# A graph layer on one core: ScalarE's column picks in three loads, turned data and the norm in steps without a layer

## The chip, the core and the metric

The kernel runs on 1 core of one Trainium2 chip. The core's engines have their own instruction streams, each in order, and wait for each other by semaphores: TensorE (PE; its weight loads are PEld), VectorE (DVE), ScalarE (ACT), GpSimd (POOL) and SyncE (SP, which only issues transfers). The metric is the device time of one execution in microseconds (us), lower is better; the number compared is the median of several runs.

## What is computed

One layer of an equivariant graph network on 12500 nodes of 128 features, with 412500 edges sorted by their target node `dst`, then a residual and a layer norm. The essence of the reference:

```python
f0 = x0 @ W1_0e / sqrt(MUL);  f1 = einsum('nui,uw->nwi', x1, W1_1o) / sqrt(MUL)
feat0, self0 = f0[:, :MUL], f0[:, MUL:];  feat1, self1 = f1[:, :MUL], f1[:, MUL:]
e0, e1 = feat0[edge_src], feat1[edge_src]                 # a gather for each edge
h = gelu(gelu(edge_scalar_attr @ W_mlp1 / sqrt(8)) @ W_mlp2 / sqrt(64))
w00, w01, w10, w11 = h @ Wp_00, h @ Wp_01, h @ Wp_10, h @ Wp_11
out0_a = w00 * e0 * ea0
out0_b = w11 * sum(e1 * ea1[:, None, :], -1) / sqrt(3)
out1_a = (w01 * e0)[:, :, None] * ea1[:, None, :]
out1_b = w10[:, :, None] * e1 * ea0[:, :, None]
n0, n1 = segment_sum(mid0, edge_dst), segment_sum(mid1, edge_dst)   # mid = concat(out) / sqrt(2)
y = [cos * self0 + sin * (n0 @ W2_0e), cos * self1 + sin * einsum(n1, W2_1o)]
out = layernorm(x + y)
```

## The kernel before

**Tiling.** The edges are cut into 806 *runs* of 512 (4 columns `q` of 128 edges) and the runs into 202 *chunks* of 4. The nodes are cut into 25 *groups* of 512 for the features before the edges and the norm behind them; the last group has 212.

**Start.** A loop over the groups loads x (SP), turns it on PE into `xT`, which stays in SBUF for the whole kernel, multiplies it by the weights `wf`, and stores the features to `table` in DRAM from ACT's queue (`store_nodes`, line 260). Meanwhile POOL gathers the rows of the first 18 runs from x itself (72 gathers); these are turned and multiplied later (`turn_rows`, `features`). The small loads (weights, first node of each chunk, and `tile_first`, the first target node of each 128 edges, in tiles `tf`) leave SP's queue one in each turn of that loop (line 925). `tile_places` (DVE) turns `tf` into offsets. Loads that are needed later stand in the list `late` and leave SP's queue in the main loop, 12 a step.

**Main loop.** Step `s` treats run `s`, with `c, k = divmod(s, 4)`. The order of the work on each engine is written out by hand (`tc.manual_schedule`): the program order of a step is what each engine does.

- POOL: `gather(s + 18)` (line 222), one indirect DMA for each column of 128 edges, from `table` into one of 19 buffers `G`. Some columns are left out because another engine makes them:
- DVE and ACT *pick columns*: for 128 edges they copy 128 columns of `xT` one by one into a tile `gt` (`pick_nodes` loads the addresses into registers, line 178; `pick` copies, line 190 on DVE and 192 on ACT). PE multiplies the tile by `wf` (line 198) and ACT copies the result to `G` (`picked_rows`, 199). `SLOTS` says how many columns each engine takes in each slot of a run: DVE 32 on average in three slots, ACT 28 in two (12 and 16). Each 128 columns save POOL one gather. SP makes one column in 14 runs with single-row transfers (`aid`).
- PE: the edge weights of coming runs (`weights`, 569), the segment sums of run `s - 1` into PSUM (`segments`, 666 and 668), and the edge network two chunks ahead: `radial` turns the edge data (527, ACT copies it out in 529), `mlp1` (536, ACT's gelu in 540), `mlp2` (551 and 556). `radial` stands in step k = 0, `mlp1` in k = 1, `mlp2` in k = 3. `turn_attributes` (521, 523) comes once in 32 runs. These small products share two PSUM buffers named `h`.
- DVE: the messages `M` of run `s` (637, 641), the indicator `own` of the next chunk (`select`, 616 and 630, which also reads one element of each gathered piece, 597), and the addition of a finished chunk's sums to the accumulator `acc` (681), which covers 768 nodes.
- Norm: `due` names the chunk after which a group is complete. Then `norm` does the group's products on PE (`moments`, 698 and 701), ACT copies them to `y` (706) and moves the remaining accumulator columns to the other `acc` buffer (`move_sums`, 428); DVE clears the rest of it piece by piece (425). Before the change this stands in step k = 3 of the next chunk, beside `mlp2`. `norm_on` (statistics, 714) and `norm_end` (normalise on ACT, 742, and a store from SP's queue, 260) follow for two groups at a time in steps 1 and 2 of the chunk after.

**End.** The last two groups, 23 and 24, are complete only with the last chunks; `end` marks the last two chunks, where the norm's steps stand earlier.

Of the kernel before, what the change touches and what calls it, by code (L numbers as in the profile page):

```python
# [50 lines left out]
SLOTS = {DVE: [(12, 12, 0), (12, 12, 8), (12, 12, 8), (12, 12, 16)], ACT: [(12, 16)]}  # L51
# [7 lines left out]
def gnn_kernel(ctx: ExitStack, tc: tile.TileContext, x, src, dst, ea4, ea8, w1_0, w1_1, wm1, wm2,  # L59
# [277 lines left out]
    def weight_loads():  # L337

        yield w1r, sub(wm1, 0, [[0, P // RAD], [HID, RAD], [1, HID]])
        yield w2b, sub(wm2, 0, [[0, 2], [HID, HID], [1, HID]])  # L340
        for j, w in enumerate((wp00, wp01, wp10, wp11)):
            yield wpb[:, j * MUL:(j + 1) * MUL], sub(w, 0, [[0, 2], [MUL, HID], [1, MUL]])
        for t, w in ((w20, w2_0), (w21, w2_1)):
            yield t[:MUL, :], w[:MUL, :]
            yield t[MUL:, :], sub(w, MUL * MUL, [[0, 3], [MUL, MUL], [1, MUL]])
        yield first_node, sub(dst, 0, [[1, 1], [CH * SB, NCH]])
        for b, t in enumerate(tile_first):
            c0, n = b * P, t.shape[0]
            last = c0 + n == NCH and E < NCH * CH * SB
            if last:  # L350
                yield (t[n - 1:n, :].rearrange("a (k o) -> a k o", o=1),
                       sub(dst, (NCH - 1) * CH * SB, [[1, 1], [0, CH * Q], [1, 1]]))
                k = -(-(E - (NCH - 1) * CH * SB) // P)
                yield t[n - 1:n, :k], sub(dst, (NCH - 1) * CH * SB, [[k * P, 1], [P, k]])
            yield t[:n - last], sub(dst, c0 * CH * SB, [[CH * SB, n - last], [P, CH * Q]])
# [37 lines left out]
    NT = -(-NCH // P)  # L393
    tile_first = [cst.tile([min(P, NCH - b * P), CH * Q], I32, name=f"tf{b}") for b in range(NT)]
# [12 lines left out]

    def tile_places():

        for b, t in enumerate(tile_first):  # L410
# [234 lines left out]
    def places(c):  # L645

        b, r = divmod(c, P)
# [37 lines left out]
    before_last = due[NCH - 1][0] - 1  # L685

    def moments(b, sums=None):
        n0, nn, full, tail, tiles = group(b)
        if not pend:
# [3 lines left out]
        j = len(pend)  # L693
        pend.append(b)
        pt = ps.tile([P, XB, P], F32, name="h")
        at = n0 - base[-1] if b in due[NCH - 1] else 0
        for t, k in tiles:
# [5 lines left out]
            else:  # L703
                nc.vector.tensor_tensor(pt[:k, t, :], pt[:k, t, :], sums[:k, t, :], op=OP.add)
        if full:
            nc.scalar.activation(Y["y"][:, j, :full, :], pt[:, :full, :], AF.Copy)
        if tail:
            nc.scalar.activation(Y["y"][:tail, j, full, :], pt[:tail, full, :], AF.Copy)

    def statistics(b):  # L710
        j = pend.index(b)
        st = wk.tile([P, XB, 6], F32, name="bst")
        for t, k in group(b)[4]:
            nc.vector.bn_stats(st[:k, t, :], Y["y"][:k, j, t, :])
# [8 lines left out]
    def normalise(last=False, keep=False):  # L723
# [9 lines left out]
        for j, b in enumerate(pend):  # L733
            if b in done:
                continue
            for t, k in group(b)[4]:
                i = j * XB + t - i0
                if last and t % 2:
                    nc.vector.tensor_scalar(y[:k, j, t, :], y[:k, j, t, :], r[:k, i:i + 1], m[:k, i:i + 1],
                                            op0=OP.mult, op1=OP.add)  # L740
                    continue
                nc.scalar.activation(y[:k, j, t, :], y[:k, j, t, :], AF.Identity,  # L742
                                     bias=m[:k, i:i + 1], scale=r[:k, i:i + 1])
            store_nodes(nc.sync, out, b, y[:, j])
# [4 lines left out]
    def norm(bs):  # L749
        for b in bs:  # L750
            moments(b)
# [14 lines left out]
    def norm_last(bs):  # L766
# [6 lines left out]
        if len(pend) > len(done):  # L773
            deviations()
            normalise(True)

# [119 lines left out]
    with tc.manual_schedule(engines={PE, ACT, DVE, SP}):  # L896
# [7 lines left out]
        for b in range(min(AHEAD, NG)):  # L904
# [9 lines left out]
                 NG // 2 + 9: tile_places, NG // 2 + 10: lambda: mlp2(1), NG // 2 + 11: make_ws, NG: make_wpost}  # L914
# [20 lines left out]
        late = list(aid_load())  # L935
# [10 lines left out]
        for s in range(NCH * CH + CH):  # L946
# [7 lines left out]
            if s % P == P // 2 and (s // P + 1) * P < NS:  # L954
# [10 lines left out]
            pick(ACT, P)  # L965
            pick_nodes(ACT, s, 1)
# [39 lines left out]
            if k == 1 and 1 < c < NCH:  # L1006
                norm_on(due.get(c - 2, []))
            if k == 2 and 1 < c < NCH - 1:
                norm_end(due.get(c - 2, []))
            if k == 0 and c == NCH:  # L1010
                norm_end(due.get(c - 3, []))
                norm_on(due.get(c - 2, []))
                norm_end(due.get(c - 2, []))
# [12 lines left out]
            if s == 2:  # L1026
                nc.vector.memset(owns[1], 0.0)
            if s == 5:
# [38 lines left out]
```

## Time and profile before

| | us |
|---|---|
| median of 3 runs (lowest to highest) | 3556.44 (3555.64 to 3560.35) |
| the profiled execution's own time | 3556.29 |
| its span, first to last instruction | 3554.4 |

A line of a group in the profile reads: line, engine, operation, output<-inputs, shape, count, then busy time in us and the mean ns of one, then the engine's idle time just ahead of them and what ended it. A line of the timeline has the start, the busy time, engine, line, operation and in brackets the idle time ahead with its releaser. A line of waits has the waiting group, what released it, total us, times and the longest. "issue" as a releaser means that the engine waited for nothing that the profile shows. ACTq, DVEq and SPq are the engines' own instruction issue (register loads, DMA starts).

### The profile page before, as it was taken

The page shows a single profiled execution, that of the slowest core. Times are in us where ns is not written, and L with a number is a line of the kernel's source. Part 1 is how long each engine was busy: PE and PEld are TensorE (multiplying, and loading weights), DVE is VectorE, ACT ScalarE, POOL GpSimd, SP SyncE. Part 2 cuts the span into 40 slices and gives each one's busy share as a digit, 9 for nine tenths or more (in the row PEclk, how much of TensorE's full clock was granted, in tenths as well). Part 3 has the DMA queues.
Part 4 walks back from the last instruction along what each step waited for, and adds up shares of the span by engine and source line. Part 5 has one row for each costly group of instructions (what it writes and reads, how often), then busy time and mean ns, then how long its engine had stood idle before and what let it go on. Part 6 is the DMA issues. An engine that isn't in the chain of part 4 may idle for free. (4 is left out here: it accounts for less than half of the span.)

```text
span 3554.4 us, 143693 instructions
## 1 busy us (share of the span) xinstructions
PE 3159.9 (89%) x28598; PEld 2755.6 (78%) x28598; DVE 3129.2 (88%) x29317; ACT 2797.6 (79%) x23671; POOL 2667.6 (75%) x2804
## 2 busy tenths in 40 slices
PE   6899898998898988998899898898899989888888
PEld 6777777787777777877788787787787777777777
DVE  2699999999999999999899899888899888889897
ACT  3488788788888888887887888877787887788785
POOL 7777777777777777777777777777777777777775
PEclk8999999998999999899998899989899999999998
DMA  8322332223322223322323323323323232232221
GB/s 199 70 62 68 63 64 65 63 61 74 64 60 67 63 60 74 64 60 62 68 61 70 67 59 64 65 63 68 65 62 64 59 69 63 60 69 63 60 65 47
DMA packets 579225, 239.29 MB, mean 67 GB/s; under 512 B 483651, under 2 KB 528747, under 8 KB 578347
## 3 DMA queue, kind: packets, MB, share of 16 engines
q0 software_dynamic: 89536, 183.55, 20.3%
q1 hardware_dynamic: 468041, 40.02, 9.1%
q10 hardware_dynamic: 20770, 6.47, 0.8%
q8 instruction: 252, 4.13, 0.5%
q14 instruction: 626, 5.13, 0.5%
HBM read 217.00 MB, written 12.80 MB: 65 GB/s over the span
## 5 line engine op out<-in xcount | busy, mean ns | idle before, releaser
L222 POOL DMA_INDIRECT G<-table,idx x2726 | 2598.9, 953 | 836.7 <-issue 718.5
L192 ACT ACTIVATE gt<-xT 128x1 f32 x22016 | 2166.7, 190 | 73.3 <-issue 53.6
L190 DVE COPY gt<-xT 128x1 f32 x25216 | 1728.6, 144 | 212.1 <-issue 172.9
L666 PE MATMUL sums<-own,M 128*128 128x96 f32 x6446 | 1354.8, 294 | 74.3 <-DVE M L641 73.0
L668 PE MATMUL sums<-own,M 128*128 128x96 f32 x6446 | 1319.7, 288 | 85.1 <-DVE M L641 84.1
L666 PEld LDWEIGHTS sums<-own,M 128*128 128x128 f32 x6446 | 1037.5, 201 | 181.9 <-DVE M L641 101.7
L668 PEld LDWEIGHTS sums<-own,M 128*128 128x128 f32 x6446 | 1035.3, 202 | 108.9 <-DVE M L641 107.6
L641 DVE TENSOR_TENSOR M<-w,G 128x384 f32<-128x384 f32 x1612 | 880.1, 547 | 0.0
L569 PE MATMUL w<-wpb,h 64*128 64x128 f32 x6448 | 649.3, 305 | 57.8 <-DVE M L641 56.3
L569 PEld LDWEIGHTS w<-wpb,h 64*128 64x128 f32 x6448 | 496.5, 197 | 199.6 <-issue 74.3
L637 DVE TENSOR_TENSOR M<-w,G 128x256 f32<-128x256 f32 x806 | 333.4, 414 | 34.4 <-issue 19.9
L540 ACT ACTIVATE h<-h 128x512 f32<-128x512 f32 x404 | 216.3, 586 | 178.6 <-PE h L536 165.7
L536 PE MATMUL h<-eT,w1b 64*128 64x128 f32 x3232 | 288.7, 319 | 8.4 <-ACT e L523 8.3
L536 PEld LDWEIGHTS h<-eT,w1b 64*128 64x128 f32 x3232 | 241.3, 218 | 38.7 <-ACT e L523 13.7
L556 ACT ACTIVATE h<-h 128x512 f32<-128x512 f32 x404 | 213.5, 577 | 26.3 <-PE h L551 22.5
L551 PE MATMUL h<-h,w2b 64*64 64x256 f32 x3232 | 222.6, 391 | 0.0
L199 ACT ACTIVATE G<-h 128x128 f32<-128x128 f32 x369 | 96.4, 277 | 120.5 <-PE h L198 76.4
L198 PE MATMUL h<-wf,gt 128*128 128x128 f32 x738 | 143.5, 294 | 1.9 <-ACT h L556 0.9
L529 ACT ACTIVATE eT<-h 128x128 f32<-128x128 f32 x202 | 56.0, 277 | 112.7 <-PE h L527 89.5
L551 PEld LDWEIGHTS h<-h,w2b 64*64 64x64 f32 x3232 | 104.5, 133 | 44.8 <-issue 0.5
L630 DVE TENSOR_TENSOR own<-oh,e 128x512 f32<-128x512 f32 x202 | 137.6, 681 | 0.7 <-issue 0.2
L681 DVE TENSOR_TENSOR acc<-sums,acc 128x384 f32 x202 | 111.2, 550 | 9.7 <-issue 6.2
(113 smaller groups left out, 1329.1 us busy)
## 6 DMA issues: line engine op xcount, KB each, us to landing
G<-table SPq DMA_DIRECT2D x7168, 0.5 KB
G<-table,idx POOLq DMA_INDIRECT x2726
e<-in_edge_attr SPq DMA_DIRECT2D x201, 64.0 KB
own<-in_x SPq DMA_DIRECT2D x24, 256.0 KB
table<-acc ACTq DMA_DIRECT2D x24, 256.0 KB
xt<-in_edge_attr SPq DMA_DIRECT2D x24, 256.0 KB
out<-y SPq DMA_DIRECT2D x24, 256.0 KB
xt<-in_dst SPq DMA_DIRECT2D x5, 256.0 KB
```

What stands on the lines that cost most here:

```text
L190: nc.vector.tensor_copy(to, col)
L192: nc.scalar.activation(to, col, AF.Copy)
L222: nc.gpsimd.indirect_dma_start(out=G[s][:, q, :], out_offset=None, in_=x if s < raw_runs else table, in_offset=bass.IndirectOffsetOnAxis(a ...
L536: nc.tensor.matmul(p1[h][:, j // 2, j % 2, :], w1b[rows, j, :], eT[c][rows, :], start=True, stop=True)
L540: nc.scalar.activation(H1[c][h], p1[h].rearrange("p k j e -> p (k j e)"), AF.Gelu_apprx_tanh, scale=1.0 / math.sqrt(RAD))
L551: nc.tensor.matmul(p2[r][k * HID:(k + 1) * HID, h * n:(h + 1) * n], w2b[rows, :], H1[c][h][rows, k * n:(k + 1) * n], start=True, stop=True)
L556: nc.scalar.activation(H2[c][r].rearrange("p k j e -> p (k j e)"), p2[r], AF.Gelu_apprx_tanh, scale=1.0 / math.sqrt(HID))
L569: nc.tensor.matmul(WP[i][:, q, :], H2[c][q % 2][rows, k, q // 2, :], wpb[rows, :], start=True, stop=True)
L637: nc.vector.tensor_tensor(M[s][:, :, :, :MUL], w[:, :, :2 * MUL].rearrange("p q (a u) -> p q a u", a=2), g[:, :, None, :MUL].to_broadcast( ...
L641: nc.vector.tensor_tensor(M[s][:, :, j, MUL:].rearrange("p q (i u) -> p q i u", i=3), w[:, :, None, (2 + j) * MUL:(3 + j) * MUL].to_broadc ...
L666: nc.tensor.matmul(flat[:, bass.ds(at, 4 * FIRST_HALF)].bitcast(F32), M[s][:, q, 0, :], own[:, 3 * WIDE:], start=False, stop=False)
L668: nc.tensor.matmul(sb[:, 1:, bass.ds(at, 4 * WIDE)].bitcast(F32), M[s][:, q, 1, :], own[:, :3 * WIDE].rearrange("p (a j) -> p a j", a=3), ...
```

## The change

1. ACT picks 28 and 32 columns by turns, in three slots: (12, 8, 8) and (12, 8, 12). The third slot's addresses are loaded ahead of the layer, its columns are copied behind it.
2. `radial` goes to step k = 2, one chunk further ahead; `turn_attributes` from the 21st to the 24th run of 32 (k = 0); `load_indices` two steps on.
3. The norm's products go to step k = 0 of the second chunk behind (`norm_products`), its copy and `move_sums` to k = 1 (`norm_keep`); the first clearing is in that same step. Statistics and end move to k = 2 of the third and k = 0 of the fourth chunk behind.
4. The products of group 23 are done by tiles of 128 nodes as soon as each is complete (`done_at`), so that one of four is left for the end; `find_first` keeps later edges from writing to finished tiles. The products of group 24 stay in PSUM and are normalised from there; its tiles are stored one by one from two queues.
5. `tile_first` is cut into tiles of 16, 128 and 58 chunks. The first is loaded first of the start's small loads, the other two behind the loads of `late`; their `tile_places` come in run 9.

```diff
-SLOTS = {..., ACT: [(12, 16)]}
+SLOTS = {..., ACT: [(12, 8, 8), (12, 8, 12)]}
+FIRST_TILES = 16
...
     def weight_loads():
+        yield from tile_loads(0)
         yield w1r, sub(wm1, 0, [[0, P // RAD], [HID, RAD], [1, HID]])
...
-        for b, t in enumerate(tile_first):
-            c0, n = b * P, t.shape[0]
+    def tile_loads(b):
+        t, c0 = tile_first[b], tile_from[b]
...
+    tile_from = [0, *range(FIRST_TILES, NCH, P)]
+    NT = len(tile_from)
+    before_last = due[NCH - 1][0] - 1
+    done_at = [math.ceil((before_last * GN + (t + 1) * P + MARGIN) / N * NCH) - 1 for t in range(XB)]
...
+        for t, (a, z) in enumerate(zip(done_at, done_at[1:])):
+            nc.vector.tensor_scalar(strays[:, a + 1:z + 1], strays[:, a + 1:z + 1], float((t + 1) * P), None, op0=OP.max)
...
-    def moments(b, sums=None):
+    def moments(b, sums=None, part=None, hold=False):
         n0, nn, full, tail, tiles = group(b)
+        if part is not None:
+            tiles = tiles[part:part + 1]
...
+        if sums is None and b == NG - 1:
+            Y["pt"] = pt
+            return
+        if part is not None:
+            nc.scalar.activation(Y["y"][:, j, part, :], pt[:, part, :], AF.Copy)
+            return
+        if hold:
+            Y["held"] = Y["y"][:, j], pt
+            return
...
+                if last:
+                    eng = nc.sync if t % 2 else nc.scalar
+                    eng.dma_start(out[b * GN + t * P:b * GN + t * P + k, :], y[:k, j, t, :])
+            if not last:
+                store_nodes(nc.sync, out, b, y[:, j])
...
     def norm(bs):
         for b in bs:
-            moments(b)
+            moments(b, part=XB - 1 if b == before_last else None)
             move_sums()
             new_sums()
+    def norm_products(bs):
+        for b in bs:
+            moments(b, hold=True)
+    def norm_keep(bs):
+        for b in bs:
+            y, pt = Y.pop("held")
+            nc.scalar.activation(y, pt, AF.Copy)
+            move_sums()
+            new_sums()
...
-        late = list(aid_load())
+        late = list(aid_load()) + [load for b in range(1, NT) for load in tile_loads(b)]
...
             pick(ACT, P)
+            if k == 1 and 1 < c < NCH - 2:
+                norm_keep(due.get(c - 2, []))
+                clearing += [(c, a) for a in range(4)] if c - 2 in due else []
             pick_nodes(ACT, s, 1)
...
-            if k == 0 and c + 2 < NCH:
-                radial(c + 2)
-            if s % ET == 21 and s - 21 + ET < NS:
+            if s == 0:
+                radial(2)
+            if k == 2 and c + 3 < NCH:
+                radial(c + 3)
+            if s % ET == 24 and s - 24 + ET < NS:
                 turn_attributes(s // ET + 1)
...
+            pick(ACT, P)
+            pick_nodes(ACT, s, 2)
             if k % 2 and c + 2 < NCH:
-                pick(ACT, P)
                 (mlp1 if k == 1 else mlp2)(c + 2)
...
-            if k == 1 and 1 < c < NCH:
+            if k == 2 and 2 < c < NCH - 1:
+                norm_on(due.get(c - 3, []))
+            if k == 0 and 3 < c < NCH - 1:
+                norm_end(due.get(c - 4, []))
+            if k == 1 and c == NCH - 1:
                 norm_on(due.get(c - 2, []))
-            if k == 2 and 1 < c < NCH - 1:
-                norm_end(due.get(c - 2, []))
...
-            if k == (1 if end else 3) and 0 < c < NCH:
+            if k == 0 and 1 < c < NCH - 2:
+                norm_products(due.get(c - 2, []))
+            if k == 1 and c == NCH - 2:
                 norm(due.get(c - 1, []))
-                clearing += [(c, a) for a in range(4)] if c - 1 in due and not end else []
+            if k == 0 and (c - 3 == done_at[0] or c - 2 in done_at[1:-1]):
+                moments(before_last, part=0 if c - 3 == done_at[0] else done_at.index(c - 2))
...
+            if s == 9:
+                tile_places(range(1, NT))
```

More of the change, by code (lines that the diff above doesn't have):

```diff
@@ L392, in gnn_kernel @@
     first_at = cst.tile([1, NCH], I32)
-    NT = -(-NCH // P)
-    tile_first = [cst.tile([min(P, NCH - b * P), CH * Q], I32, name=f"tf{b}") for b in range(NT)]
+    tile_from = [0, *range(FIRST_TILES, NCH, P)]
+    NT = len(tile_from)
+    tile_first = [cst.tile([z - a, CH * Q], I32, name=f"tf{b}")
+                  for b, (a, z) in enumerate(zip(tile_from, tile_from[1:] + [NCH]))]
+    before_last = due[NCH - 1][0] - 1
+    assert len(due[NCH - 1]) == 1
+    done_at = [math.ceil((before_last * GN + (t + 1) * P + MARGIN) / N * NCH) - 1 for t in range(XB)]
+    assert due[done_at[-1]] == [before_last] and done_at == sorted(set(done_at))
+    assert not any(c in due for c in (*range(done_at[0] - 1, done_at[-1]), 0, NCH - 4, NCH - 2)) and done_at[-1] < NCH - 2
     def find_first():
@@ L645, in places @@
     def places(c):
-        b, r = divmod(c, P)
+        b = max(b for b, a in enumerate(tile_from) if a <= c)
+        r = c - tile_from[b]
         _, PLACE[c] = nc.values_load_multi_w_load_instructions(
@@ L692, in moments @@
             nc.vector.memset(Y["v"], 1.0)
-        j = len(pend)
-        pend.append(b)
+        if b not in pend:
+            pend.append(b)
+        j = pend.index(b)
         pt = ps.tile([P, XB, P], F32, name="h")
@@ L775, in norm_last @@
             normalise(True)
+        Y.pop("pt")
     odd_f = cst.tile([1, 1], F32)
```

44 lines of the change are left out of this document (23 added, 21 removed).

## The prediction

> **What bounds the kernel now.** I read the page first: shares, then the costliest groups.
>
> ```profile
> span 3554.4 us, 143693 instructions
> PE 3159.9 (89%) x28598; PEld 2755.6 (78%) x28598; DVE 3129.2 (88%) x29317; ACT 2797.6 (79%) x23671; POOL 2667.6 (75%) x2804
> ...
> L222 POOL DMA_INDIRECT G<-table,idx x2726 | 2598.9, 953 | 836.7 <-issue 718.5
> L192 ACT ACTIVATE gt<-xT 128x1 f32 x22016 | 2166.7, 190 | 73.3 <-issue 53.6
> ```
>
> By shares PE and DVE look like the limit and POOL like the idlest engine. But of POOL's 836.7 us of idle, 718.5 is "issue": time in which it waits for nothing. So I asked for POOL's waits (total us, times, longest) and then for the gathers themselves (ns shortest/median/longest, first and last start).
>
> ```profile
> POOL G L222 <- issue: 740.2, 2427, 0.3
> POOL G L222 <- DVE M L641: 50.2, 147, 5.7
> ```
> ```profile
> L222 POOL DMA_INDIRECT G<-table,idx x2726: 938/944/1508, 99.4 to 3528.3; - x195
> L222 POOL DMA_INDIRECT G<-in_x,idx_raw x72: 940/944/1091, 3.8 to 92.7; - x72
> ```
>
> 740.2 us over 2427 gaps is 0.305 us each, never above 0.3 as printed: a fixed gap that belongs to the gather. The second row's 147 gaps are the same 0.3 (50.2 less one of 5.7 leaves 0.305 for each of 146). So POOL stops once, and else issues a gather every (3528.3 - 99.4) / 2725 = 1.258 us from 99.4 to 26 us before the end. **POOL's gathers set the time**; a gather left out is worth 1.258 us as long as the engines behind keep up. Do they? Two tables count DVE's messages (L637, one for each run of 512 edges) and POOL's gathers in the same stretches: the stretch, its length, busy time with the count in brackets, PE's clock, DMA share, GB/s.
>
> ```profile
> 0.00:200.00 200.00, 9.94 (x24) 0.93 0.56 126
> 200.00:1000.00 800.00, 78.69 (x190) 0.93 0.30 65
> 1000.00:1800.00 800.00, 78.19 (x189) 0.95 0.30 64
> 1800.00:3400.00 1600.00, 152.66 (x369) 0.93 0.30 64
> ```
> ```profile
> 0.00:200.00 200.00, 144.73 (x152) 0.93 0.56 126
> 200.00:1000.00 800.00, 606.06 (x637) 0.93 0.30 65
> 1000.00:1800.00 800.00, 606.04 (x637) 0.95 0.30 64
> 1800.00:3400.00 1600.00, 1212.05 (x1273) 0.93 0.30 64
> ```
>
> Gathers run at one pace throughout. The first 18 runs take the 72 gathers from x, the other 788 take 2726, or 3.459 each. At 200 us POOL has done 18 + (152 - 72) / 3.459 = 41 runs and DVE 24: a lead of 17. At 1800 us it is 409 against 403, at 3400 us 777.5 against 772: about 6. So the consumers start 17 runs behind, work at 800 / 190 = 4.21 us a run, catch up, and from about 1800 us go at POOL's pace, 1600 / 369 = 4.34. What holds them at 4.21 is DVE (busy time of PE, PEld, DVE, ACT, POOL in one stretch, then DVE's largest wait in it):
>
> ```profile
> 200.00:1000.00 800.00, 721.50 (x6614) 630.54 (x6615) 736.80 (x7020) 660.10 (x5686) 606.06 (x637) 0.93 0.30 65
> ```
> ```profile
> DVE gt L190 <- issue: 40.0, 115, 0.6
> ```
>
> In that stretch DVE is busy 736.8 us and loads registers for 40.0 more, 97% together; PE has 721.5 (90%), ACT 660.1 (83%). So every wait of ACT or PE that goes is worth nothing directly, and I look for what the change does to POOL's queue and to the two ends.
>
> **The change part by part.**
>
> *Columns.* ACT picks 28 columns a run now (22016 / 128 = 172 groups), then 28 and 32 by turns. By the code's own rule for placing groups this makes 184. Each group replaces one gather: 12 gathers x 1.258 = **15.1 us** less on POOL. It adds 1536 columns to ACT. The group's row says 190 ns for one, but 2166.7 / 22016 = 98 ns of busy time: neighbours overlap. So 151 us on ACT, beside POOL's work; 12 more products on PE and copies on ACT (0.5 and 0.3 us each) are lost in this. The third register load:
>
> ```profile
> L178 ACTq TENSOR_LOAD <-pick x1696: 306/808/1850, 143.9 to 3516.2; - x189
> ```
>
> Two loads of 12 and 16 become three of 8 to 12. All 1696 loads cost ACT 53.6 us of visible gaps (the page's row), 0.03 us each, because columns already queued cover them; a load of 16 outlasts that cover most. I take nothing for 794 more loads. From both sides: 53.6 us gained if the gaps go, 794 x 0.81 = 643 us of ACT lost if no load is covered. (The Trainium skill, DMA: Bandwidth & Descriptors, "Latency and other measured facts", gives a register load a floor of about 600 ns, which speaks against splitting one: by it 794 more are about 476 us of ACT, the estimate near which rival B's time would lie, where by the rows the sum stands. The shortest load here took 306 ns, so the floor does not hold in this trace; whether the loads stay covered is B.)
>
> *Start.* Where is POOL's one stop, and what must land before it?
>
> ```profile
> 56.37 1.36 SPq L925 DMA_DIRECT2D tf<-in_dst  x1
> ...
> 65.16 1.58 SPq L925 DMA_DIRECT2D tf<-in_dst  x2
> ```
> ```profile
> 72.73 0.69 DVE L304 COPY acc<-w 128x512 f32<-128x512 f32 x1 [7.60 <-PE w L301]
> ...
> 81.27 0.38 ACTq L260 DMA_DIRECT2D table<-acc  x1
> ...
> 97.05 0.62 ACTq L262 DMA_DIRECT2D table<-acc  x1
> ...
> 99.37 0.94 POOL L222 DMA_INDIRECT G<-table,idx  x1 [5.68 <-DVE M L641]
> ```
>
> Run 18 is the first that reads `table`, so it waits for the last store into it (97.05); the DVE named had long nothing to do with it, as run 18's buffer is unused. The stores come from ACT in order, and the one at 81.27 had its data at 73.42: 7.85 us late. Ahead of it stand the `tf` loads, single 4-byte elements: 128x16 and 73x16 in the two large ones. I read it as waiting for one of these. The change loads 16 rows (256 elements) there and the other 186 behind the pick loads. If 5.38 us or more of the 7.85 go, POOL's stop (5.68 less the usual 0.30) goes whole: **5.4 us**; below, nothing goes. I take 5.4. What is late next is run 19's buffer, which run 0's messages free; those move forward with the same chain. The moved loads pass 33 pick and index loads (16 more than now) on SP; behind them wait only edge loads for the second chunk: 0 to some 5 us for the consumers, not POOL.
>
> *Steps without a layer.*
>
> ```profile
> ACT y L706 <- PE h L701: 111.9, 24, 7.6
> ```
> ```profile
> DVE acc L425 <- ACT acc L428: 14.0, 7, 4.7
> ```
> ```profile
> SPq L260 <- ACT y L742: 180.9, 24, 20.2
> ```
> ```profile
> 2384.13 2.74 DMA e<-in_edge_attr
> ```
>
> Edge data are now turned in step 2 of a chunk, attributes and the norm's products in step 0, and the norm's copy one step after its products. PE and ACT do the same work; ACT's 111.9 us in front of the copy mostly go, worth nothing in time but room for the 151 us above. What is queued behind the copy on ACT is that step's columns and first layer. Edge data now have 3 steps (13 us) instead of 5 between load and use, and land in 2.74 us; SP's stores, moved two steps, can hold the load behind them (20.2 us at worst), then PE waits some us in the consumers' time. The one new risk: clearing the spare accumulator on DVE (L425) now follows in the *same* step as ACT's move out of it (L428), where it came two steps behind the products. Bounds for each of the 23: 0 to 4.7 us, the longest now; I take 0.5, near what 14.0 / 23 gives today. It comes out of the consumers' reserve (below): no time. Some 15 small DVE operations come to runs 1 and 9, none longer than the 0.69 us of the large copy above: under 10 us of the same reserve, while POOL is 17 runs ahead.
>
> *End.*
>
> ```profile
> 3528.14 0.25 PE h L698 x2
> 3528.39 0.89 PE h L701 x8
> ...
> 3532.63 0.65 PE w L569 x8
> ```
> ```profile
> 3536.21 0.42 DVE L637 TENSOR_TENSOR M<-w,G 128x256 f32<-128x256 f32 x1 [5.08 <-PE w L569]
> ...
> 3546.57 0.29 DVE L714 BATCH_NORM_STATS2 bst<-y 128x6 f32<-128x128 f32 x1 [1.94 <-ACT y L706]
> ...
> 3549.97 0.72 SPq L262 DMA_DIRECT2D out<-y  x1
> ```
>
> After POOL's last gather PE works without a break: four tiles of the last but one norm group, 0.25 + 0.89 = 1.14 us each, stand ahead of weights that DVE waits for (5.08). Three of the four are done chunks earlier: 3 x 1.14 = **3.4 us**. The last gather (3528.32 + 0.94, then about 2.5 to land) is there by 3531.8, before DVE would want it at 3534.7, so it does not fill the gap. The last group is read from PSUM: about 0.4 us for the copies before L714. Its two stores leave by two queues: about 0.7 us, the second issue. End: **4.5 us**, between 3 and 7.
>
> *Sum* against the profiled execution's 3556.3 us (0.1 below the median, 3556.4): 15.1 + 5.4 + 4.5 = 25.0, so 3531 us.
>
> **The consumers' reserve.** After, POOL needs 2714 / 788 x 1.2569 (1600 / 1273) = 4.329 us a run; DVE unhindered 4.21. Over 3300 us the consumers could gain 3300 x (1 - 4.21 / 4.329) = 91 us; closing the lead from 17 to 6 takes 11 x 4.33 = 48. So they may lose about 43 us before the end feels it.
>
> **The rivals.**
>
> A, *DVE waits for ACT's move*, the slower side. With w us in each of 23 groups instead of today's 14.0 in all, the time is 3531 + max(0, 23w - 14 - 43). Nothing up to w = 2.5; within 0.2% of now from 3.3; slower from 3.9. At the longest wait seen, 4.7, it is 3582. For it: same step. Against: the seven waits average 2.0, and products without a layer ahead of them end earlier.
>
> B, *ACT becomes the bound*. Today 660.1 / 190 = 3.47 us busy and 0.74 idle a run; with columns 3.66. If the third load shows with 0.5 us (between its 0.31 and 0.81) and half of the idle stays, 4.53 a run: about 788 x 4.53 + 99 + 26 = 3695. It decides when the idle plus what shows of the loads passes 0.6 us a run. Against: ACT's idle is mostly waiting for PE, and shrinks as ACT gets work.
>
> C, *the change does not do what it says at the ends*: the stop stays or comes back as a wait for buffers, PE has other work at the end. Only the 15.1: 3541.
>
> **How the numbers follow.** Forecast 3531: 0.69. C: 0.15. A: 0.09 (0.03 within 0.2%, 0.06 slower). B: 0.07 (0.03, 0.04). Faster by over 0.2% (7 us, about what a measurement of this kernel can tell from no change) 0.84, within 0.06, slower 0.10. The range runs from 3523 (an end 3 us shorter, 5 us of longer gathers fewer) to 3550, which takes in C and A up to w = 3.3.
>
> **What would show it.** Right: 2714 gathers from `table`, still 1.258 us apart, first near 94, last near 3508, 23 us or less to the end; ACT near 2950 us busy, hardly any wait of L706; a lead that still falls to about 6 runs. Wrong: POOL waiting for M, or a lead above 10 runs at the end (A or B; the DVE wait of L425 and ACT's waits tell which); a first gather from `table` at 99 or a last product late (C).

## The result, and the profile after

The changed kernel takes **3537.79 us** (median of 5 runs, 3534.20 to 3542.81) against 3556.44 us before (5 runs, 3553.46 to 3560.35): a ratio of **0.9950**, 95% interval 0.9937 to 0.9963, or 13 to 22 us less. The profiled execution took 3534.96 us, 21.3 us less than that of before (3556.29). The experiments below ran on four chips; on three of them the kernel before took 3553.75 to 3555.56 us. The fourth granted 0.70 to 0.74 of TensorE's clock instead of about 0.93, the kernel before took 5612 us there, and the four runs on it are compared only with that.

The page of the changed kernel: span, shares, and the two groups on which the forecast rested. Lines have moved: the gather is now L223, ACT's pick L193, its load L179.

```profile
span 3533.2 us, 146063 instructions
PE 3151.8 (89%) x28622; PEld 2746.0 (78%) x28622; DVE 3130.8 (89%) x29324; ACT 2940.8 (83%) x25220; POOL 2656.1 (75%) x2792
L223 POOL DMA_INDIRECT G<-table,idx x2714 | 2587.1, 953 | 830.6 <-issue 716.5
L193 ACT ACTIVATE gt<-xT 128x1 f32 x23552 | 2306.5, 192 | 58.6 <-issue 46.6
```

ACT has 143 us more to do, as forecast (151). Its visible gaps at the register loads did not grow with 771 more loads: 46.6 us, 53.6 before. The shares tell nothing of the gain; the gathers do. First their row (ns shortest/median/longest, first and last start), then the three in POOL's timeline that came late (start, busy time, and in brackets the idle time ahead):

```profile
L223 POOL DMA_INDIRECT G<-table,idx x2714: 940/944/1493, 94.2 to 3510.6; - x194
```
```profile
166.16 0.94 POOL L223 DMA_INDIRECT G<-table,idx  x1 [1.18 <-ACT gt L193]
...
171.53 0.94 POOL L223 DMA_INDIRECT G<-table,idx  x1 [1.93 <-ACT G L604]
...
188.11 0.94 POOL L223 DMA_INDIRECT G<-table,idx  x1 [0.64 <-issue]
```

The last gather starts 17.7 us earlier (3510.6 for 3528.3): 12 gathers fewer, 15.1; the first one from `table` 5.15 earlier (94.22 for 99.37); less 2.84 in these three gaps (1.18 + 1.93 + 0.64, less the usual 0.305 each), which did not exist before; 0.3 is left over. From the last gather to the end of the span it is now 22.5 us, 26.1 before: 3.6. Together 21.3.

How near are the consumers? The two count tables of the prediction, for the changed kernel: DVE's messages (L653), then POOL's gathers.

```profile
0.00:200.00 200.00, 9.95 (x24) 0.93 0.56 127
200.00:1000.00 800.00, 78.34 (x189) 0.94 0.30 65
1000.00:1800.00 800.00, 78.77 (x190) 0.94 0.30 64
1800.00:3400.00 1600.00, 154.47 (x373) 0.93 0.30 64
```
```profile
0.00:200.00 200.00, 146.68 (x154) 0.93 0.56 127
200.00:1000.00 800.00, 605.75 (x638) 0.94 0.30 65
1000.00:1800.00 800.00, 605.96 (x637) 0.94 0.30 64
1800.00:3400.00 1600.00, 1212.38 (x1272) 0.93 0.30 64
```

With 2714 / 788 = 3.444 gathers a run, POOL leads by 14 runs at 1000 us (11 before), 9 at 1800 us (6) and 5.4 at 3400 us (5.5). The consumers still catch up, but much later: most of their reserve is used.

The waits on which the steps without a layer bear (total us, times, longest), and the tail in the timeline:

```profile
PE h L199 <- ACT eT L545: 108.6, 78, 2.5
...
DVE acc L441 <- ACT acc L444: 29.3, 11, 5.2
...
ACT y L799 <- PE h L720: 14.6, 16, 2.8
```
```profile
3515.07 0.42 DVE L653 TENSOR_TENSOR M<-w,G 128x256 f32<-128x256 f32 x1 [1.75 <-PE w L585]
...
3527.40 0.46 ACT L774 ACTIVATE y<-h,rs 128x128 f32<-128x128 f32 x1 [1.03 <-DVE rs L763]
...
3527.89 0.41 DVE L771 TENSOR_SCALAR y<-h,rs 84x128 f32<-84x128 f32 x1 [0.53 <-ACT y L774]
3528.33 0.36 SPq L778 DMA_DIRECT2D out<-y  x1
```

ACT's 111.9 us ahead of the norm's copy have become 14.6. A new wait of about the same size stands on PE, which now comes to `picked_rows` right behind `radial` and waits for its copy; E1 below has the same order and shows no cost of it. Near the end DVE waits 1.75 us for weights instead of 5.08. But the last two normalisations, which ran side by side, now run one behind the other: DVE waits 0.53 us for ACT. Both now read the same PSUM tile; whether that is the reason is not shown.

### The profile page after: what moved, and what is told of

The parts are those of the page before. It is cut to its first block, busy times and chain, and to the rows that moved or that the text cites. A ratio compares the mean times of both kernels' runs of the same rounds, so it can differ in the third digit from the quotient of the medians.

```text
span 3533.2 us, 146063 instructions
## 1 busy us (share of the span) xinstructions
PE 3151.8 (89%) x28622; PEld 2746.0 (78%) x28622; DVE 3130.8 (89%) x29324; ACT 2940.8 (83%) x25220; POOL 2656.1 (75%) x2792
## 4 chain that ended last, share of the span: by engine, by line
DVE 48%; issue 10%; PE 10%; SPq 10%; ACT 7%; DVEq 5%; POOL 5%; DMA 4%; ACTq 1%; POOLq 0%
DVE gt L191 26%; DVE M L657 12%; SPq L210 7%; ACT gt L193 5%; DVEq L179 5%; POOL G L223 5%; DVE M L653 4%; DMA G<-table,idx 3%; PE sums L683 2%; PE sums L685 2%; SPq L206 2%; DVE acc L698 2%; PE w L585 1%; PE h L567 1%; DVE own L646 1%
## 5 line engine op out<-in xcount | busy, mean ns | idle before, releaser
L223 POOL DMA_INDIRECT G<-table,idx x2714 | 2587.1, 953 | 830.6 <-issue 716.5
L193 ACT ACTIVATE gt<-xT 128x1 f32 x23552 | 2306.5, 192 | 58.6 <-issue 46.6
L585 PEld LDWEIGHTS w<-wpb,h 64*128 64x128 f32 x6448 | 488.0, 198 | 232.0 <-DVE M L657 96.5
L556 ACT ACTIVATE h<-h 128x512 f32<-128x512 f32 x404 | 219.3, 595 | 205.5 <-PE h L552 179.3
L653 DVE TENSOR_TENSOR M<-w,G 128x256 f32<-128x256 f32 x806 | 333.9, 414 | 35.9 <-issue 16.8
L572 ACT ACTIVATE h<-h 128x512 f32<-128x512 f32 x404 | 219.3, 595 | 99.4 <-PE h L567 72.8
L199 PE MATMUL h<-wf,gt 128*128 128x128 f32 x762 | 171.1, 309 | 113.1 <-ACT eT L545 108.6
L552 PE MATMUL h<-eT,w1b 64*128 64x128 f32 x3232 | 253.9, 301 | 0.0
L567 PE MATMUL h<-h,w2b 64*64 64x256 f32 x3232 | 242.9, 420 | 0.0
L552 PEld LDWEIGHTS h<-eT,w1b 64*128 64x128 f32 x3232 | 213.6, 202 | 20.6 <-issue 3.6
L199 PEld LDWEIGHTS h<-wf,gt 128*128 128x128 f32 x762 | 122.7, 203 | 135.5 <-ACT eT L545 125.7
```

The costliest lines, as they stand in the source:

```text
L193: nc.scalar.activation(to, col, AF.Copy)
L199: nc.tensor.matmul(pt, GT.pop((e, i)), wf, start=True, stop=True)
L223: nc.gpsimd.indirect_dma_start(out=G[s][:, q, :], out_offset=None, in_=x if s < raw_runs else table, in_offset=bass.IndirectOffsetOnAxis(a ...
L552: nc.tensor.matmul(p1[h][:, j // 2, j % 2, :], w1b[rows, j, :], eT[c][rows, :], start=True, stop=True)
L567: nc.tensor.matmul(p2[r][k * HID:(k + 1) * HID, h * n:(h + 1) * n], w2b[rows, :], H1[c][h][rows, k * n:(k + 1) * n], start=True, stop=True)
L585: nc.tensor.matmul(WP[i][:, q, :], H2[c][q % 2][rows, k, q // 2, :], wpb[rows, :], start=True, stop=True)
```

## The experiments

Theory: POOL's gathers, 1.258 us each, and the two ends set the time; the moved steps give none. Rivals: the moves themselves gave the time; the consumers (DVE, or ACT) are or become the bound. Lines in a profile of an experiment are those of its own code.

### One part at a time

**E1**, the changed kernel with the old 28 columns.

```diff
-ACT: [(12, 8, 8), (12, 8, 12)]}
+ACT: [(12, 16)]}
```

> The changed kernel with ACT's old 28 columns a run in two loads; the moved steps, the start and the end stay changed. Theory (POOL's gathers, 1.258 us each, plus the two ends set the time; the moved steps give none of their own): 12 gathers come back, 2726 from table, so 15 us above the changed kernel: about 3551 to 3553 us. Rival (the moved steps gave the time, by ending waits of ACT and DVE): near 3538 us, as with 30 columns.

**E2**, the kernel before with the new columns alone.

```diff
-ACT: [(12, 16)]}
+ACT: [(12, 8, 8), (12, 8, 12)]}
...
+            pick(ACT, P)
+            pick_nodes(ACT, s, 2)
             if k % 2 and c + 2 < NCH:
-                pick(ACT, P)
```

> The kernel before with only the 30 columns in three loads. Theory: 2714 gathers from table, 15.1 us less, about 3541 us, with POOL's stop at 99 us and 26 us after the last gather as before; the lead still falls to about 6 runs, so the moves were not needed for it. Rival (the moved steps made the room that the columns need): consumers fall behind, POOL waits for M or the last message comes late, 3545 to 3556 us.

**E3**, the kernel before with the new start alone.

```diff
+FIRST_TILES = 16
+        yield from tile_loads(0)
-        late = list(aid_load())
+        late = list(aid_load()) + [load for b in range(1, NT) for load in tile_loads(b)]
+            if s == 9:
+                tile_places(range(1, NT))
```

> The kernel before with only the shorter tf load at the start and the rest of tf behind the pick loads. Theory: POOL's stop of 5.7 us goes, first table gather near 94.2; if POOL's waits for buffers at 166 to 188 us (3.7 us less the usual gaps, 2.8 lost) come from the start itself, 2.4 us less, 3554 us; if they come from the moved steps or the third slot, they are absent here and it is 5.2 us less, 3551 us.

**E4**, the kernel before with the new end alone (`done_at`, products by tiles, `rows_of`, tile stores, as in the diff above).

```diff
+            if k == 0 and (c - 3 == done_at[0] or c - 2 in done_at[1:-1]):
+                moments(before_last, part=0 if c - 3 == done_at[0] else done_at.index(c - 2))
```

> The kernel before with only the end changed: three of the four tiles of the last but one norm group done chunks earlier, the last group read from PSUM, its stores tile by tile on two queues. Theory: last gather to end 26.1 us becomes 22.5, so 3.6 us less, about 3553 us. Rival (the end was shorter only because of the moved steps around it): 26 us stay, 3556 us. DVE's final normalise should again stand behind ACT's by about 0.5 us.

All four shared 30 runs of the kernel before, median 3553.75 us:

| | median us | ratio, 95% interval | us against before, by the ratio | expected |
|---|---|---|---|---|
| E1 moves, start, end | 3544.47 | 0.9975 (0.9964 to 0.9985) | -8.9 | -3 to -5 |
| E2 columns | 3546.98 | 0.9982 (0.9973 to 0.9992) | -6.4 | -15.1 |
| E3 start | 3548.42 | 0.9983 (0.9974 to 0.9992) | -6.0 | -2.4 or -5.2 |
| E4 end | 3551.41 | 0.9994 (0.9985 to 1.0003) | -2.1 | -3.6 |

Start and end alone give 8.1 together, E1, which has the moves as well, 8.9. Each of these figures is uncertain by some 3 us, so by the times alone the moves could be worth up to some 6 us either way; E4 alone can't be told from no change. The profiles say more: E1's gathers keep E3's pace, its end is 0.5 us shorter than E4's, and nothing else is left for the moves. So the rival that the moves gave the 18.7 us falls; that the consumers are the bound falls by POOL's pace, 1.256 to 1.259 us a gather in all four. E1's time itself lies between the two forecasts, and E2's inside the range of its rival. But E1 is better than expected and E2 worse: the *columns* are worth some 9 us beside the rest and 6 alone, not 15. Whether the moves help the columns can't be told from these two figures, whose uncertainties are some 6 and 3 us. The gathers of E1, E3, E4 and E2, in this order, and E2's stop:

```profile
L223 POOL DMA_INDIRECT G<-table,idx x2726: 940/944/1489, 94.0 to 3520.5; - x195
```
```profile
L223 POOL DMA_INDIRECT G<-table,idx x2726: 940/944/1497, 93.7 to 3519.6; - x195
```
```profile
L222 POOL DMA_INDIRECT G<-table,idx x2726: 938/944/1489, 100.6 to 3523.8; - x195
```
```profile
L222 POOL DMA_INDIRECT G<-table,idx x2714: 940/944/1507, 104.7 to 3519.4; - x194
```
```profile
104.73 0.94 POOL L222 DMA_INDIRECT G<-table,idx  x1 [11.36 <-DVE M L641]
```

With the new start the first gather from `table` comes at 94.0 and 93.7, and no gap in POOL's timeline of E1 or E3 is above the usual 0.3. So the start is worth its whole 5.4 us there. With the old start POOL's stop differs from kernel to kernel: 5.68 us in the profile of before, 7.08 in E4, 11.36 in E2, where SP has 32 loads of pick addresses to issue instead of 16. That accounts for most of what E2's profile misses of the 15.1 us: the first gather from `table` comes 5.4 us later than before, waits for buffers cost 2.8 and the end is 2.4 longer, while shorter gathers give 2.0 back. The consumers did not fall behind: at 3400 us POOL leads by 5 runs. E4's span ends 22.4 us after its last gather, as the theory has it (26.1 before), and E1's 21.9.

Where do the columns lose? The starts of runs 13, 14 and 15 on DVE, in the changed kernel, in E1 and in E3:

```profile
147.53 0.42 DVE L653 TENSOR_TENSOR M<-w,G 128x256 f32<-128x256 f32 x1 [1.96 <-issue]
156.16 0.42 DVE L653 TENSOR_TENSOR M<-w,G 128x256 f32<-128x256 f32 x1 [4.50 <-issue]
163.12 0.42 DVE L653 TENSOR_TENSOR M<-w,G 128x256 f32<-128x256 f32 x1 [2.52 <-issue]
```
```profile
143.55 0.42 DVE L653 TENSOR_TENSOR M<-w,G 128x256 f32<-128x256 f32 x1 [1.90 <-issue]
150.58 0.42 DVE L653 TENSOR_TENSOR M<-w,G 128x256 f32<-128x256 f32 x1 [2.91 <-issue]
157.35 0.42 DVE L653 TENSOR_TENSOR M<-w,G 128x256 f32<-128x256 f32 x1 [2.33 <-issue]
```
```profile
143.32 0.42 DVE L646 TENSOR_TENSOR M<-w,G 128x256 f32<-128x256 f32 x1 [3.03 <-issue]
150.36 0.42 DVE L646 TENSOR_TENSOR M<-w,G 128x256 f32<-128x256 f32 x1 [2.91 <-issue]
155.40 0.42 DVE L646 TENSOR_TENSOR M<-w,G 128x256 f32<-128x256 f32 x1 [0.61 <-issue]
```

And runs 0 and 15 in the kernel before, and run 0 in the changed kernel:

```profile
98.40 0.42 DVE L637 TENSOR_TENSOR M<-w,G 128x256 f32<-128x256 f32 x1
...
165.37 0.42 DVE L637 TENSOR_TENSOR M<-w,G 128x256 f32<-128x256 f32 x1 [0.62 <-issue]
```
```profile
91.77 0.42 DVE L653 TENSOR_TENSOR M<-w,G 128x256 f32<-128x256 f32 x1
```

From run 13 to 14 it is 8.6 us with 30 columns (9.1 in E2) and 7.0 with 28: ACT's first columns fall into the runs in which it still copies turned rows. From 14 to 15 it is 7.0 and 6.8 with the moves, 5.0 without; from 7 to 8 in the same way 5.6 and 3.9; from 12 to 13 the moves win 1.1. And run 0's message comes at 91.8 in the changed kernel, at 87.8 and 88.3 in E1 and E3. Each of these is small, and together they make run 15 start 6 to 8 us later than in E1 and E3. Its buffer is the one that POOL's late gather at 166.16, the first of run 34, waits for (19 buffers). That the copies of turned rows are what holds run 14 is read from the code: the profile puts these waits down to "issue".

The waits for buffers are not the columns' alone. E4, with 28 columns and neither the moves nor the new start, has two of them, and E2, with 30 columns and no moves, four in the same stretch (here its longest), all ahead of the first gathers of runs 33 to 35 and 39:

```profile
175.43 0.94 POOL L222 DMA_INDIRECT G<-table,idx  x1 [1.00 <-ACT G L596]
191.97 0.94 POOL L222 DMA_INDIRECT G<-table,idx  x1 [0.48 <-issue]
```
```profile
181.11 0.94 POOL L222 DMA_INDIRECT G<-table,idx  x1 [1.92 <-ACT G L588]
```

In these six profiles the waits go with how long after POOL's first gather from `table` the message of run 15 starts: 61.7 us in E3, 63.3 in E1 and 66.0 in the kernel before, all without a wait in this stretch; 66.5 in E4, 68.0 in E2 and 68.9 in the changed kernel, which lose 0.87, 2.3 and 2.84 us. So the kernel before had next to no margin left here.

So, in the profiles, the changed kernel is 9.2 us ahead of E1 (spans 3533.2 and 3542.4): 15.1 for the gathers, less 2.84 for the waits for buffers, 2.0 for longer gathers (below; no edit explains them), 0.9 at the two ends (0.2 left over).

### Loads at the start

By the code, 30 columns need 32 loads of pick addresses from SP, 28 columns 16, 32 columns 4. I took these loads for the reason of the late first message.

**E10**, the changed kernel with 4 late loads a step.

```diff
-            for _ in range(min(12, len(late))):
+            for _ in range(min(4, len(late))):
...
+            if s == 9:
+                addresses()
```

> The changed kernel (30 columns) with the 37 late loads on SP issued 4 a step instead of 12. Theory (the 32 pick loads in a row hold up run 0's chain): first message near 88 us instead of 91.8, POOL's waits for buffers between 160 and 190 us under 1 us in all instead of 2.8, 2 to 3 us less than the changed kernel: 0.993 to 0.995 of before. Rival (the early loss is from the moved steps and the third slot alone): first message near 92 us, POOL waits as in the changed kernel.

Measured: 3550.86 us (12 runs, 3540.74 to 3559.33), before 3554.33, ratio 0.9988 (0.9978 to 0.9998). The first message was at 93.9 us, and POOL lost far more than 2.8 us. Three of its nine gaps above 1 us between 143 and 208 us, and a wait of DVE:

```profile
163.83 0.94 POOL L222 DMA_INDIRECT G<-table,idx  x1 [3.76 <-ACT gt L192]
172.32 0.94 POOL L222 DMA_INDIRECT G<-table,idx  x1 [5.06 <-issue]
181.79 0.94 POOL L222 DMA_INDIRECT G<-table,idx  x1 [4.78 <-ACT gt L192]
```
```profile
DVE off L429 <- DMA tf<-in_dst: 10.6, 2, 6.5
```

The theory of this experiment fell, and a better one came out of it. SP ran ahead of the other engines, so fewer loads a step did not spread the first 27, which left from 67 to 86 us; but the last five, with `tf` behind, now stand behind the first transfers of `aid`, whose addresses DVE makes in run 5. SP waited 26.4 us for these addresses, and `tf` left it at 130 us instead of 87. DVE waited 10.6 us for `tf`, run 20's message came 19.7 us later than in the changed kernel (204.8 for 185.1), and POOL's nine gaps cost 21.2 us (2.84 there). The profiled run is 21.3 us longer than the changed kernel's; it is one of the longest of its twelve. **What the consumers lose in the first 20 runs, POOL loses too, nearly us for us, once its margin to the buffers is gone.**

**E12**, the changed kernel with the second half of the pick addresses loaded at runs 40 to 47.

```diff
+            if s == 40:
+                late = list(aid_load(1))
-            for _ in range(min(12, len(late))):
+            for _ in range(min(12 if s < 40 else 2, len(late))):
```

> The changed kernel (30 columns) with the loads of the second half of the pick rows (16 of 32, used only after run 500) at runs 40 to 47 instead of at the start. Theory (the number of pick loads at the start delays run 0's chain: first message at 85.5 us with 4 loads, 87.8 and 88.3 with 16, 91.8 and 93.9 with 27 to 32): first message at 87.5 to 88.5 us, POOL's lost time on buffers between 160 and 190 us falls from 2.8 us to 0.5 or less, the last gather starts near 3508 us, 0.992 to 0.995 of before, 2 to 3 us better than the changed kernel. Rival (it is chance from one execution to the next): first message above 90 us, waits as before.

Measured: 3534.12 us (5 runs, 3531.95 to 3537.58), before 3555.56, ratio 0.9942 (0.9928 to 0.9955): not to be told from the changed kernel. First message at 93.55 us, and the same gaps:

```profile
166.32 0.94 POOL L225 DMA_INDIRECT G<-table,idx  x1 [1.08 <-ACT gt L195]
171.69 0.94 POOL L225 DMA_INDIRECT G<-table,idx  x1 [1.93 <-ACT G L606]
188.15 0.94 POOL L225 DMA_INDIRECT G<-table,idx  x1 [0.48 <-issue]
```

A miss, but the gaps are now seen in two executions, at the same places, so they are not chance. The number of loads alone does not set the first message: 85.5 and 85.9 us with 4 of them (E9, E11), 87.8 and 88.3 with 16 (E1, E3), 91.8 with 32, but 93.6 here with 16. It may still have a share: here SP came to these loads (`aid_at` first) only at 64.67 us, where it was 61.40 to 62.78 in those five, and counted from there the message takes 23.0 and 23.1 us with 4 loads, 25.4, 26.1 and here 28.9 with 16, 30.4 with 32. DVE and ACT wait for a pick load by 7.7 and 4.2 us in this profile. What makes these loads late stays open.

### More columns

**E9**, 32 columns in each run.

```diff
-ACT: [(12, 8, 8), (12, 8, 12)]}
+ACT: [(12, 8, 12)]}
```

> 32 columns in each run (12, 8, 12), on a chip that grants about 0.93 of the clock: 2701 gathers from table, and by the way 4 loads of pick rows at the start instead of 32. Theory (gathers set the time while the consumers keep up; the 32 loads make the first message 4 us late and POOL wait): 16.4 us for 13 gathers and 2.8 us for the waits less than the changed kernel, 0.9885 to 0.9905 of before, some 3515 to 3520 us; run 0's message near 88 us, no wait for buffers above 0.5 us, the consumers' lag at run 800 between 17 and 25 us. Rival (the third load eats the gain, or the consumers are already the bound): 0.994 of before or more, lag at run 800 above 30 us.

Measured: **3678.74 us** (3676.61 to 3696.66), ratio 1.0364 (1.0346 to 1.0382). Two columns more and the kernel is some 140 us slower. The busy times of 200 to 1000 us (PE, PEld, DVE, ACT, POOL), in the changed kernel and in E9, then E9's messages in that stretch and two waits of its DVE:

```profile
200.00:1000.00 800.00, 722.18 (x6609) 629.37 (x6606) 733.96 (x6986) 693.58 (x6037) 605.75 (x638) 0.94 0.30 65
```
```profile
200.00:1000.00 800.00, 709.41 (x6285) 611.39 (x6284) 701.57 (x6660) 700.94 (x6127) 589.13 (x619) 0.90 0.27 63
```
```profile
200.00:1000.00 800.00, 75.07 (x181) 0.90 0.27 63
```
```profile
DVE acc L441 <- ACT acc L444: 135.4, 23, 7.9
...
DVE M L653 <- PE w L585: 40.7, 40, 2.1
```

Now POOL is not the bound: it does 619 gathers instead of 638. ACT's own account points to why, busy and idle time a run:

| ACT's columns | busy | idle | pace of the consumers | pace of POOL if not held |
|---|---|---|---|---|
| 28 (before) | 660.1 / 190 = 3.47 | 0.74 | 4.21 | 4.35 |
| 30 (changed) | 693.6 / 189 = 3.67 | 0.56 | 4.23 | 4.33 |
| 32 (E9) | 700.9 / 181 = 3.87 | 0.55 | 4.42 | 4.31 |

(POOL: gathers a run x 1.258.) From 28 to 30 columns ACT's new work went into its idle time. From 30 to 32 the idle time no longer shrinks and the work is added to the pace, past POOL's. Of the three steps tried, 30 columns are the last before the edge. The third load is not what shows: ACT's visible gaps at its loads are 5.1 us in this stretch, 10.4 in the changed kernel. But something else changed with the columns: in all runs of E9 and E11 the granted clock was 0.89 to 0.90, against 0.93 to 0.94 in the kernel before on the same two chips, and PE's busy time a run rose from 722.18 / 189 = 3.82 to 709.41 / 181 = 3.92 us. Whether the lower clock is part of the cause or follows from the slower pace is not shown.

DVE's wait that grew most in E9 is rival A's, the clear behind ACT's move: 135.4 us.

**E11**, E9 with the clears two steps later.

```diff
-            if k == 1 and clearing and c < NCH:
+            if k == 3 and clearing and c < NCH:
```

> 32 columns in each run, and the four clears of the spare accumulator two steps later (step 3 of a chunk instead of step 1, where ACT's move stands). With 32 columns alone it was 3679 us (1.0364 of before), DVE waited 135.4 us in 23 clears for ACT's move, and the messages went at 4.42 us a run in 200 to 1000 us. Theory A (this wait is what makes the consumers slow): it falls below 15 us, the messages go at about 4.29 us a run or faster, and the time falls by 105 us or more, to 3570 us or less (1.005 of before or less). Theory B (ACT with its columns and its waits for PE is the bound; the clear only shows it): the wait turns up elsewhere, as DVE's wait for weights from PE, the pace stays above 4.35 us and the time above 3640 us (1.024).

Measured: 3683.84 us (3676.36 to 3698.43), ratio 1.0360 (1.0343 to 1.0378). The wait for the move is gone from the list, and the messages go at 800 / 179 = 4.47 us a run. What grew instead, and the engines of the chain that ended last:

```profile
DVE M L653 <- PE w L585: 130.6, 65, 6.0
```
```profile
ACT 40%; PE 31%; DVE 9%; issue 7%; SPq 4%; ACTq 3%; POOL 3%; DMA 2%; DVEq 1%; POOLq 0%
```

The wait moved and the time stayed: it only showed that ACT is late. DVE has 9% of the chain, 48% in the changed kernel. So at 32 columns rival A falls, and what is left is rival B, ACT with its waits for PE, at the lower clock; which of these waits keeps the 0.55 us a run was not tried.

### On the chip with the lower clock

E0 is the changed kernel itself; E5 and E9 are the same kernel, E8 and E10 too; E6 takes `ACT: [(12, 10, 12)]`.

> The changed kernel once more, beside the next three. About 3535 to 3538 us against 3554 to 3556 before. If its early loss belongs to it and not to one execution, run 0's first message is again near 92 us (88 in the two kernels with 28 columns and the new start), the step from run 13 to 14 again takes 8.6 us (7.0 there), and POOL again waits for buffers, 3 us or so in all, between 160 and 190 us.

> The changed kernel with 32 columns in each run (12, 8, 12): 2701 gathers, and by the way 4 loads of pick rows at the start instead of 32. Theory (gathers set the time while the consumers keep up; the 32 loads are what makes the first message 4 us late and POOL wait): 13 gathers x 1.258 = 16.4 us less, run 0's message near 88 us, no wait for buffers (2.8 us less), 3519 to 3523 us; the consumers' lag behind POOL, 17 us at the end now, grows to at most 25. Rival (the third load and the longer ACT eat the gain, or the consumers are already the bound): 3535 us or more, lag at the end above 30 us.

> The changed kernel with 34 columns in each run (12, 10, 12): 2689 gathers, 36 loads of pick rows. Theory: 25 gathers x 1.258 = 31 us less for POOL, but the consumers at 4.21 to 4.25 us a run end no earlier than some 3515 us, so most of the second half of the gain is lost: 3515 to 3525 us, lag at the end above 25 us, first message at 92 us and POOL's waits for buffers as with 30 columns. If gathers alone set the time: 3506 us. If ACT's picks become the bound: above 3537 us.

> The changed kernel with the 37 late loads on SP issued 4 a step instead of 12 a step (the pick addresses are made at run 9 instead of 5). Theory (the 32 pick loads in a row hold up what stands behind them, ACT's copy at 88 us among it): first message near 88 us instead of 92, POOL's waits for buffers shrink from 2.8 us to under 1, so 2 to 3 us less than the changed kernel. Rival (the early loss is from the moved layer steps and the third slot alone): first message stays near 92 us, same time as the changed kernel.

Against the kernel before on that chip: E0 1.0123 (1.0096 to 1.0151), E5 1.0034 (1.0008 to 1.0060), E8 1.0129 (1.0107 to 1.0151), E6 1.1618 (1.1594 to 1.1642). None of the expectations can be judged from them. E0's gathers and its ACT's largest wait:

```profile
L223 POOL DMA_INDIRECT G<-table,idx x2714 | 2566.9, 946 | 2943.6 <-issue 1321.4
```
```profile
ACT gt L193 <- issue: 1286.1, 2103, 1.8
```

A gather takes what it always takes (946 ns), but POOL is idle for more than half of the span and ACT stands 1286 us at the picks whose addresses it has just loaded, where it stood 46.6 us. These are 2103 gaps of 0.61 us on average, near the length of one load (median 0.565 us, 0.566 on the other chip): the loads take no longer, and it looks as if what covered them there does not cover them here. There the change is a loss of 1.2%, and the four times go roughly with this wait of ACT: 940 us in E5, 1265 in E8, 1286 in E0, 2305 in E6. The kernel before has no profile on that chip, so that its loads cost it less is not shown.

## Why the prediction was right, and where it was not

The forecast was 3531 us; the median is 6.8 above it, the profiled run 4.0. In the profile the sum of 25.0 us became 21.3: 15.1 for the columns, 2.3 left of the start, 3.6 for the end and 0.3 left over. The mechanism was right, and the start is the term that was mis-sized most.

- **The bound.** Right: gathers are 1.256 to 1.259 us apart before, after and in E1 to E4, and what differs in time is found in POOL's row and in the end behind its last gather.
- **Columns, 15.1 us.** The 12 gathers went, as counted, and POOL kept its pace, but their net is 9 us (changed kernel against E1) or 6 (E2 against before). Beside the rest of the change, 2.84 us went to waits for buffers, since the columns make early runs later, 2.0 to longer gathers that no edit explains; alone, 5.4 went to the old start's longer stop. The 2.84 us are one loss: they are booked to the start below, but E1 has the start without them.
- **The third load at nothing.** Right at 30 columns (46.6 us of gaps). The prediction had weighed the Trainium skill, DMA: Bandwidth & Descriptors, "Latency and other measured facts", with its floor of about 600 ns for a register load; the shortest here is 306 ns again, and the loads stay hidden.
- **Start, 5.4 us.** The stop went, as E3 shows alone. The step that failed is the sentence "What is late next is run 19's buffer, which run 0's messages free; those move forward with the same chain." Run 0's message did move by 6.6 us (98.40 to 91.77), but run 15's only by 2.25 (165.37 to 163.12), against 5.15 for POOL. With the start alone the sentence holds: in E3 run 15 moves by 10.0 (to 155.40). With the columns and the moves beside it, it does not. The margin was used up, and 2.84 us came back as waits for buffers, ahead of runs 34, 35 and 39. So 2.3 were left of 5.15. The sentence that the moved and added loads cost the consumers up to 5 us, "not POOL", failed with it: E10 shows that in this stretch such a loss is POOL's. The reading that the late store waited for `tf` is half tested: E3 moves `tf` and the stop goes, but the profile of before has a pick load at the end of ACT's 10.13 us of idle there.
- **Steps without a layer, no time.** Right, as far as E1 can tell. The clear's wait is 29.3 / 23 = 1.3 us a group, not 0.5, inside its bounds. It doesn't come from the shared step alone: 10.2 us in E1, with the same steps and 28 columns, 4.0 in E2, with 30 columns and the old steps, 29.3 with both.
- **End, 4.5 us.** 3.6 in the changed kernel, 3.8 in E4. The products and the copies came as priced; the 0.7 for two queues did not: from the start of the last normalisation to the end of the span it is 5.8 us, 5.5 before, with L771 waiting for L774.
- **Reserve, 43 us.** Enough: the lead falls to 5.4 runs. But the edge was 2 columns away, and there it was not DVE that was short of time: DVE has 9% of E11's chain, ACT 40%.
- **Rivals.** C happened by half: the stop came back as a wait for buffers, 2.84 of 5.15 us. A did not decide, not even at 32 columns (E11). B did not happen at 30 columns; at 32 something like it did, at 3679 us. That this is near its price, 3695, is luck: the price was for 30 columns with 0.5 us of the loads showing in each run, and in E9 0.03 us show (5.1 / 181). Its condition was put at 0.6 us a run; by the prediction's own figures it is 4.33 - 3.66 = 0.67.

## What to carry to other kernels

Where an engine with a fixed pace sets the time, work taken off it pays in full only while the others keep their margin at every point: here a lead of 19 buffers is long in the steady part and has no slack in the first 40 runs, so count the margin there before pricing the start. When columns, rows or tiles are shifted to a helper, write down its busy and idle time per unit for each step of the shift: here the shift was free as long as the idle time shrank, and at the step where it stopped shrinking the kernel became 3.6% slower than before. The largest new wait of a slow kernel may only mark who is late; take it away before believing it.

## What was not expected of the hardware

- Most gathers take 944 ns, but 90 to 108 of some 2700 take over 1000 ns, up to 1.5 us (E11, with 128 of them, left out). The mean is 951 ns in E4's profile, 952 in E1 and E3, 953 in those of before and after, 954 in E10 and E12. One ns is 2.7 us of the kernel's time, so 8 us lie between these profiles with no edit that explains them: as much as a term of the sum.
- The old start has a stop of 5.7, 7.1 and 11.4 us in the profiles of three kernels; E4 has the same code as the kernel before up to there, so these 1.4 us lie between executions. E3, without the stop, spreads over 5.4 us in 11 runs, E4 and E2, with it, over 7.2 and 8.8 in 11; that the stop is the reason is not shown, and E10, with only 1.3 us ahead of its first gather from `table`, spreads over 18.6.
- On the chip with 0.72 of the clock the loss is no matter of TensorE alone: in E0's profile DVE, ACT and POOL, which have no matmul, stand in "issue" for over 1200 us each, and the kernels come out in another order. Why instructions come late there stays open.
